# Four-layer network on one core: later weights prepared in nine steps, and attention's norm with tokens on partitions

## The chip, the cores and the metric

The program runs on one NeuronCore of a Trainium2 chip. Five engines share it and work through their own instruction streams, each in order: TensorE (PE: matrix products and transposes, into PSUM), VectorE (DVE), ScalarE (ACT), GpSimd (POOL) and SyncE (SP, which here only starts DMA transfers). They wait for each other through semaphores. The metric is the time of one execution on the device in microseconds (us); less is better.

## What is computed

The input is 4 images of 96 channels, 64 x 64 pixels: 16384 tokens of 96 channels. Four layers follow each other. Layer 0 is a two-layer Mamba block with a pointwise fusion. The change touches layers 1 and 2 and the weights of layers 1 to 3. In short:

```python
# layer 1: depthwise 7x7 convolution, layer norm, MLP
h = conv7x7(x) + conv_b
h = layernorm(h) * ln_g + ln_b
x = x + layer_scale * (gelu(h @ w1 + b1) @ w2 + b2)

# layer 2: attention without softmax, then a feed-forward with fp8 operands
t = tokens(x)                                   # (4, 4096, 96)
q, k, v = split(_ln_t(t) @ Wqkv + bqkv)         # 6 heads of 16
attn = einsum('bhnd,bhmd->bhnm', q, k) * D**-0.5
t = t + einsum('bhnm,bhmd->bhnd', attn, v) @ Wff + bff
t = t + qffn(_ln_t(t))                          # operands rounded to fp8

# layer 3: Fourier mixing over the 4096 tokens, then the same feed-forward
h = relu(bn1(_ln_t(t) @ w1.T))
X = fft(h); y = real(ifft(relu(X * diag + bias)))
t = t + bn2(y @ w2.T)
t = t + qffn(_ln_t(t))
```

`_ln_t` subtracts each token's mean over the 96 channels and divides by the root of its variance plus 1e-5.

## The kernel before

`t` holds the residual stream on chip, 96 channels on partitions and 16384 tokens along them. A block is 512 tokens (`MB`); there are 32 blocks, 8 to a batch (`NB`).

**Order.** In layers 1 to 3 a `manual_schedule` fixes the order of PE, DVE, ACT and POOL as the program is written. SP is not among them: the framework's scheduler places the transfers in SP's queue.

**Layer 1's convolution** (`layer1`, lines 909 to 993). First 16 chunks of `t` are built from layer 0's result (L929 to L933) and transposed into `xt`, which has rows of pixels on 128 partitions. Then 24 groups of four channels run, `g` from 0 to 23. Each group loads a 1 MB band matrix (`load(g)`, L957, three buffers), does 16 matmuls (L983 and L986) into one of four `cv` banks, and evicts four channels, on ACT in even groups (L993) and on DVE in odd ones (L991).

**The later weights** (`consts2`, L821 to L904). Before group 8 the program calls `consts2`, which loads and prepares what layers 1 to 3 need: the MLP's folded bias (three products at L836), its scaled weights, attention's weights, the two feed-forwards' weights rounded to fp8 (L860, L864; both use the same raw buffers `raww1` and `raww2`), the two batch norms folded into `a_w1` and `a_w2` (two products at L899), and the Fourier tables. All of it stands in one place in every engine's order.

**Layer 2** (`layer2`, L1102 to L1217). One loop over slots `j` runs three norms one after the other: of attention (blocks 0 to 31), of the feed-forward (32 to 63), and of layer 3 for the first batch (64 to 71). Each is spread over three slots by `norm_steps`: `center(j)` multiplies by a centring matrix (PE, L1084) and squares (ACT, L1086); `scale(j-1)` sums the squares over channels (PE, L1090) and takes the root by Ln and Exp (ACT, L1092 and L1093); `norm(j-2)` multiplies (DVE, L1096). Channels stay on partitions, so the mean and the root of each token are present on all 96 of them.

Attention is linear, so it needs only the Gram matrix of each batch's normed tokens, with a column of ones for the biases. `turn(j-3)` transposes a normed block to tokens on partitions (PE L1131, ACT L1133), and `products(j-4)` adds it to the Gram matrix (PE L1141). After a batch's last block the five steps of `weights` turn that matrix into one 97 x 96 matrix, through small products (L1147) and copies (L1157 to L1173). `out(j-4-lag)`, with `lag` = `NB` + 3, applies it to a block and adds it to `t` (PE L1179, DVE L1181). The feed-forward's `hidden` (L1236 to L1240) and `project` (L1246 to L1252) begin 35 and 37 slots in.

**Layer 3** (`fourier`) begins with `w1` (PE L1326), which reads all eight normed blocks of the first batch from `h3`.

Names that the prediction uses: `w1raw`, `bn_rows` and `a_w2raw` are raw weights on their way in `consts2`; `cv_ps` the convolution's banks; `xc_ps`, `v_ps` and `rs` the old norm's centred block, its sums of squares and its roots; `av` a tile of layer 3 that ACT scales by a value per partition (L1376); `st` and `mv` layer 1's statistics (L1006, L1007), whose roots are L1011 and L1012, and whose normed block goes back through L1025.

Of the kernel before, what the change touches and what calls it, by code (L numbers as in the profile page):

```python
# [9 lines left out]
F32 = mybir.dt.float32  # L10
# [9 lines left out]
NT = B * L  # L20
# [82 lines left out]
class Net:  # L103
# [715 lines left out]


    def consts2(self, wk, small):  # L821
        tc, nc, ins = self.tc, self.nc, self.ins
        pool = self.pool2

        def load(name, shape, dtype=F32):
            t = pool.tile(shape, dtype, name=name)
            nc.sync.dma_start(t, ins[name])
            return t


        self.c_w1 = load("c_w1", [C, HID])
        self.c_w2 = load("c_w2", [128, 3, C])
        self.c_b1 = pool.tile([128, 3], F32, name="c_b1s")
        ps = small(128, 4)
        for m in range(3):
            nc.tensor.matmul(  # L836
                ps[:, m : m + 1], self.c_w1[:, m * 128 : (m + 1) * 128], self.v("c_ln_b"), start=True, stop=True
            )
        nc.vector.tensor_add(self.c_b1, self.v128("c_b1", 0, 3), ps[:, :3])
        nc.vector.tensor_scalar_mul(self.c_w1, self.c_w1, self.v("c_ln_g"))  # L840
        ls = wk.tile([128, C], F32, name="ls_row")
        nc.sync.dma_start(ls, ins["ls_row"].partition_broadcast(128))
        for m in range(3):
            nc.vector.tensor_mul(self.c_w2[:, m, :], self.c_w2[:, m, :], ls)
        self.c_b2 = pool.tile([C, 1], F32, name="c_b2s")
        nc.vector.tensor_mul(self.c_b2, self.v("c_b2"), self.v("c_ls"))


        self.wkv = load("wkv", [C + 1, 2 * C])
        self.wqt = load("wqt", [C, C + 1])  # L850
        self.wff = load("wff", [C, C])
        self.mask = load("mask", [C, C])


        self.ffn = {}
        for k in ("f2", "f3"):
            a = wk.tile([C, HID], F32, name="w1raw", tag="raww1")
            nc.sync.dma_start(a, ins[f"{k}_w1"])
            w1 = pool.tile([C, HID], F8, name=f"{k}w1q")
            nc.vector.tensor_copy(w1, a, saturate=False)  # L860
            a = wk.tile([128, 3, C], F32, name="w2raw", tag="raww2")
            nc.sync.dma_start(a, ins[f"{k}_w2"])
            w2 = pool.tile([128, 3, C], F8, name=f"{k}w2q")
            nc.vector.tensor_copy(w2, a, saturate=False)  # L864
            b1 = pool.tile([128, 3], F32, name=f"{k}b1q")
            b2 = pool.tile([C, 1], F32, name=f"{k}b2q")
            for b, src in ((b1, self.v128(f"{k}_b1", 0, 3)), (b2, self.v(f"{k}_b2"))):
                q = wk.tile(list(b.shape), F8, name="bq", tag=f"bq{b.shape[0]}{k}")
                nc.vector.tensor_copy(q, src, saturate=False)
                nc.vector.tensor_copy(b, q)  # L870
            self.ffn[k] = (w1, w2, b1, b2)


        self.a_w1 = load("a_w1", [C + 1, NF])
        rows = wk.tile([C + 1, 4, NF], F32, name="bn1_rows")
        nc.sync.dma_start(rows, ins["bn1_rows"].partition_broadcast(C + 1))
        s1 = wk.tile([C + 1, NF], F32, name="bn1_s")
        nc.scalar.activation(s1, rows[:, 3, :], AF.Sqrt, bias=self.eps[: C + 1])
        nc.vector.reciprocal(s1, s1)
        nc.vector.tensor_mul(s1, s1, rows[:, 0, :])  # L880
        nc.vector.tensor_mul(self.a_w1[:C], self.a_w1[:C], s1[:C])
        shift = wk.tile([C + 1, NF], F32, name="bn1_b")
        nc.vector.tensor_mul(shift, s1, rows[:, 2, :])
        nc.vector.tensor_sub(self.a_w1[C:], rows[C:, 1, :], shift[C:])
        r = self.rsqrt(pool, self.v("v2"), "bn2_r")
        self.s2 = pool.tile([C, 1], F32, name="bn2_s")
        nc.vector.tensor_mul(self.s2, r, self.v("g2"))
        self.b2 = pool.tile([C, 1], F32, name="bn2_b")
        nc.vector.tensor_mul(self.b2, self.s2, self.v("m2"))
        nc.vector.tensor_sub(self.b2, self.v("be2"), self.b2)  # L890

        raw = wk.tile([C, NF], F32, name="a_w2raw")
        nc.sync.dma_start(raw, ins["a_w2"])
        gain = wk.tile([C, C], F32, name="bn2_d")
        nc.vector.tensor_scalar_mul(gain, self.ident[:C, :C], self.s2)
        self.a_w2 = pool.tile([C, 2, C], F32, name="a_w2s")
        for half in range(2):
            ps = small(C, C)
            nc.tensor.matmul(ps, raw[:, half * C : (half + 1) * C], gain, start=True, stop=True)  # L899
            nc.vector.tensor_copy(self.a_w2[:, half], ps)  # L900
        self.dft1 = load("dft1", [N1, 2 * 65])
        self.twid = load("twid", [128, 2, 2 * 65])
        self.dft2 = load("dft2", [128, 3 * 128])
        self.dft64 = load("dft64", [128, 2, 128])  # L904

    def layer1(self, scratch, t):
        tc, nc, ins = self.tc, self.nc, self.ins  # L910
# [3 lines left out]
        with ExitStack() as ctx:  # L914
# [4 lines left out]
            with (  # L919
# [48 lines left out]
                def small(rows, cols):  # L968
                    ps = psum.tile([128, 4, 128], F32, name="w_ps", tag="xt", bufs=4)
                    return ps.rearrange("p a c -> p (a c)")[:rows, :cols]  # L970

                x2 = [outer(0)]
                for g in range(C // GC):
                    if g == 8:
                        self.consts2(wk, small)
                    if g % 2 == 0 and g + 2 < C // GC:
                        x2.append(outer(g // 2 + 1))
                    w = load(g)
                    ps = psum.tile([128, GC, B, NR], F32, name="cv_ps", tag="cv", bufs=4)
                    for d in range(GC):  # L980
                        c = g * GC + d
                        for k, j in enumerate((1, 0, 2)):
                            nc.tensor.matmul(  # L983
                                ps[:, d], w[:, d, j], xt[:, c, :, 1 + j : 1 + j + NR], start=k == 0, stop=False
                            )
                        nc.tensor.matmul(ps[:, d], w[:, d, 3], x2[g // 2][:, g % 2 * GC + d], start=False, stop=True)  # L986
                    for d in range(GC):
                        c = g * GC + d
                        dst = xt[:, c, :, 2 : 2 + NR]
                        if g % 2:  # L990
                            nc.vector.tensor_scalar_add(dst, ps[:, d], cb[:, c : c + 1])  # L991
                        else:
                            nc.scalar.activation(dst, ps[:, d], AF.Identity, bias=cb[:, c : c + 1])  # L993
# [82 lines left out]
    def norm_steps(self, t, wk, psum):  # L1076
# [20 lines left out]

        return center, scale, norm

    def layer2(self, t, h3):  # L1102
# [4 lines left out]
        with ExitStack() as ctx:  # L1107
# [9 lines left out]
            for k in range(2):  # L1117
                h = wk.tile([C + 1, L], F32, name=f"h{k}")
                nc.gpsimd.memset(h[C:], 1.0)
                hs.append(h)  # L1120
            ht, gram, g = {}, {}, {}

            def block(i):
                b, s = divmod(i, NB)
                return hs[b % 2][:, s * MB : (s + 1) * MB]

            def turn(i):
                h = block(i)
                ps = psum.tile([128, 4, C + 1], F32, name="ht_ps", tag="ht")
                for d in range(4):  # L1130
                    nc.tensor.transpose(ps[:, d], h[:, d * 128 : (d + 1) * 128], self.ident[: C + 1, : C + 1])  # L1131
                ht[i] = wk.tile([128, 4, C + 1], F32, name="ht", tag="hts", bufs=2)
                nc.scalar.copy(ht[i], ps)  # L1133

            def products(i):
                b, s = divmod(i, NB)
# [45 lines left out]

            lag = NB + 3
            steps = []
            for j in range(2 * n + NB + 2):
                if 0 <= j - 1 < 2 * n + NB:
                    scale(j - 1)
                if j < 2 * n + NB:  # L1190
                    center(j)
                i = j - 2
                if 0 <= i < n:
                    norm(i, block(i)[:C])
                elif n <= i < 2 * n:
                    norm(i, xq(i - n), saturate=False)
                elif i >= 2 * n:
                    norm(i, h3[:C, (i - 2 * n) * MB : (i - 2 * n + 1) * MB])
                if 0 <= j - 4 < n:
                    products(j - 4)  # L1200
                    if (j - 4) % NB == NB - 1:
                        steps = weights((j - 4) // NB)
                else:
                    for f in steps[:1]:
                        f()
                    steps = steps[1:]
                if 0 <= j - 3 < n:
                    turn(j - 3)
                for f in steps[:2]:
                    f()  # L1210
                steps = steps[2:]
                if 0 <= j - 4 - lag < n:
                    out(j - 4 - lag)
                if 0 <= j - n - 5 < n:
                    project(j - n - 5)
                if 0 <= j - n - 3 < n:
# [465 lines left out]
```

## Time and profile before

Three runs took 3753.5, 3758.2 and 3759.5 us, a median of 3758.2.

| | |
|---|---|
| profiled execution: time | 3751.0 us |
| its span | 3749.2 us |
| PE busy | 3115.1 us (83%) |
| DVE busy | 2981.6 us (80%) |
| ACT busy | 2720.5 us (73%) |
| POOL busy | 2566.7 us (68%) |

The profile page cuts the span into 40 slices of 93.7 us and gives the busy share of each engine in tenths (9 is 90% or more), and the TensorE clock that was granted, in tenths of full speed:

```
PE   7887888788878887888887888657799997999888
DVE  5999999999999999999999999931662493444649
ACT  6887888888888888888888888541345685656557
POOL 1899989898999899989989998811001174434527
PEclk8999899899989998999999899658899999999999
```

Layer 0 fills the first 26 slices. The convolution's matmuls run from 2511.0 to 2628.6 us, layer 1's MLP to 2840, layer 2 from there to 3108, layer 3 to the end. "Busy" means that an instruction was executing; a share is an average over stages that have different limits, so what a stage is bound by is read from its own stretch. A wait is given as: engine and line that waited, what ended the wait, us in total, how often, and the longest.

### The profile page before, as it was taken

What the parts mean: (1) busy time and instruction counts of PE and PEld (TensorE: products, weight loads), DVE (VectorE), ACT (ScalarE), POOL (GpSimd) and SP (SyncE); (2) the same over time, 40 slices, a digit from 0 to 9 for tenths busy, and PEclk for the clock granted to TensorE, in tenths of its full rate; (3) what the DMA queues carried; (4) which work ended last, traced back from release to release, by engine and by line L of the source; (5) the groups of instructions that cost most, each with busy time, mean ns of one, the idle gap of its engine ahead of it and who ended that gap; (6) DMA issues with size and microseconds to landing.
All of it is one profiled execution on the core that took longest, in us unless ns stands there. A gap on an engine that the chain in (4) does not pass through costs nothing. (4 is left out here: it accounts for less than half of the span.)

```text
span 3749.2 us, 46836 instructions
## 1 busy us (share of the span) xinstructions
PE 3115.1 (83%) x15326; PEld 1404.9 (37%) x15326; DVE 2981.6 (80%) x2644; ACT 2720.5 (73%) x5456; POOL 2566.7 (68%) x922
## 2 busy tenths in 40 slices
PE   7887888788878887887888888657799997999888
PEld 3232223223222322232233233147344435676643
DVE  5999999999999999999999999931662493444649
ACT  6887888888888888888888888541345685656557
POOL 1899989898999899989989998811001174434527
PEclk8999899899989998999999899658899999999999
DMA  7656665666565666666665666376000000011001
GB/s 187 156 152 160 166 161 148 165 160 172 145 170 152 173 149 169 157 157 161 166 165 142 172 157 173 91 214 217 1 0 1 1 1 6 24 35 46 24 11 57
DMA packets 171644, 446.63 MB, mean 119 GB/s; under 512 B 48756, under 2 KB 50750, under 8 KB 168064
## 3 DMA queue, kind: packets, MB, share of 16 engines
q1 hardware_dynamic: 171400, 443.64, 45.7%
q8 instruction: 121, 1.98, 0.2%
q14 instruction: 123, 1.01, 0.1%
HBM read 369.97 MB, written 73.50 MB: 118 GB/s over the span
## 5 line engine op out<-in xcount | busy, mean ns | idle before, releaser
L648 POOL TENSOR_TENSOR hs<-hs,crep 128x2048 f32<-128x2048 f32 x384 | 1601.2, 4185 | 224.2 <-DVE hs L643 176.4
L610 ACT ACTIVATE da<-ddb,nega 128x1024 f32<-128x1024 f32 x576 | 661.5, 1149 | 197.7 <-DMA ddb<-dd 124.3
L643 DVE TENSOR_TENSOR_SCAN hs<-da,state,rep 128x1024 f32<-128x1024 f32 x288 | 669.2, 2338 | 39.6 <-PE rep L594 21.9
L621 POOL TENSOR_TENSOR up<-udb,brep 128x1024 f32<-128x1024 f32 x192 | 453.0, 2360 | 73.1 <-DMA udb<-ud 58.9
L665 PE MATMUL y<-hs,sel_r 128*32 128x512 f32 x3072 | 459.6, 692 | 12.8 <-POOL hs L648 12.3
L599 PE MATMUL rep<-dbl,sel_b 32*128 32x512 f32 x768 | 250.1, 730 | 215.1 <-DVE hs L643 215.0
L507 ACT ACTIVATE uta<-delta,bt 128x192 f32<-128x192 f32 x1024 | 381.1, 446 | 0.0
L287 PE MATMUL ps<-n,w_x 97*64 97x512 f32 x1536 | 353.8, 602 | 13.0 <-ACT xc L411 12.1
L643 DVE TENSOR_TENSOR_SCAN hs<-da,state,u 128x1024 f32<-128x1024 f32 x144 | 338.1, 2348 | 23.9 <-PE y L665 8.2
L643 DVE TENSOR_TENSOR_SCAN hs<-dap,state,up 128x1024 f32<-128x1024 f32 x144 | 335.2, 2328 | 0.5 <-ACT dap L610 0.5
L594 PE MATMUL rep<-ident,uta 128*128 128x128 f32 x1536 | 222.6, 287 | 105.6 <-DVE hs L643 93.2
L594 PEld LDWEIGHTS rep<-ident,uta 128*128 128x128 f32 x1536 | 174.9, 146 | 246.5 <-issue 133.3
L636 DVE TENSOR_TENSOR u<-udb,rep 128x1024 f32<-128x1024 f32 x192 | 235.4, 1226 | 24.8 <-DMA udb<-ud 11.4
L1240 POOL CAST hq<-y 128x1536 fp8e5<-128x1536 f16 x64 | 94.0, 1469 | 218.1 <-issue 122.6
L643 DVE TENSOR_TENSOR_SCAN hs<-da,rep 128x1024 f32<-128x1024 f32 x96 | 217.9, 2282 | 21.2 <-PE rep L594 14.8
L610 ACT ACTIVATE dap<-ddb,nega 128x1024 f32<-128x1024 f32 x192 | 214.8, 1119 | 24.9 <-DVE hs L643 24.4
L636 DVE TENSOR_TENSOR rep<-udb,rep 128x1024 f32<-128x1024 f32 x192 | 232.0, 1208 | 0.0
L287 PEld LDWEIGHTS ps<-n,w_x 97*64 97x64 f32 x1536 | 103.8, 137 | 260.2 <-issue 210.0
L665 PEld LDWEIGHTS y<-hs,sel_r 128*32 128x32 f32 x3072 | 73.7, 118 | 335.2 <-issue 257.7
L599 PEld LDWEIGHTS rep<-dbl,sel_b 32*128 32x128 f32 x768 | 65.8, 205 | 353.6 <-issue 295.2
L658 PE MATMUL y<-xc,dp 128*128 128x512 f32 x192 | 125.7, 743 | 31.3 <-ACT bt L463 31.3
L1379 POOL TENSOR_TENSOR av<-av,ec 128x780 f32<-128x780 f32 x32 | 58.8, 1837 | 133.7 <-ACT av L1376 133.7
(275 smaller groups left out, 6201.3 us busy)
## 6 DMA issues: line engine op xcount, KB each, us to landing
udb<-ud SPq DMA_DIRECT2D x768, 128.0 KB
ddb<-dd SPq DMA_DIRECT2D x768, 128.0 KB
crep<-cd SPq DMA_DIRECT2D x512, 128.0 KB
dd<-delta SPq DMA_DIRECT2D x64, 384.0 KB
band<-in_band SPq DMA_DIRECT2D x24, 1024.0 KB
ud<-delta SPq DMA_DIRECT2D x62, 384.0 KB
brep<-cd SPq DMA_DIRECT2D x128, 128.0 KB
x<-in_x SPq DMA_DIRECT2D x32, 384.0 KB
```

Source lines behind the costliest of these rows:

```text
L287: nc.tensor.matmul(ps[rows], w[:, 64 * p : 64 * p + 64], rhs[:, at.start + shift : at.stop + shift], start=k == 0, stop=k == len(ws) - 1, ...
L507: nc.scalar.mul(m["uta"][:, q, :, 32 * s4 : 32 * s4 + 32].rearrange("t (p j) d -> t p j d", p=3), m["udt"][:, :, q].rearrange("t p (j d) - ...
L594: nc.tensor.transpose(x[:, q * 128 : q * 128 + 128], made[k]["uta"][:, q, 2 * h + j], self.ident)
L599: nc.tensor.matmul(x[:, at], sel_b[rows, g], made[k]["dbl"][rows, at], start=True, stop=True)
L610: nc.scalar.activation(da, made[k]["dd", h, j], AF.Exp, scale=nega[:, col : col + 1])
L621: nc.gpsimd.tensor_mul(up, made[k]["ud", p][:, j], made[k]["brep", GP])
L636: nc.vector.tensor_mul(u, made[k]["ud", h][:, j], x)
L643: nc.vector.tensor_tensor_scan(hs[:, 1:], made[k].pop(("da", t)), u, st, ALU.mult, ALU.add)
L648: nc.gpsimd.tensor_mul(hs[:, :, :T], hs[:, :, 1:], twice(made[k]["crep", g]))
L658: nc.tensor.matmul(y, dp[:, items[k][2], p], made[k]["xc"][:, p], start=True, stop=True)
L665: nc.tensor.matmul(made[k]["y", p][row : row + 32], sel_r, made[k]["hs", p, g][:, j, at], start=False, stop=True, skip_group_check=True,)
L1240: nc.gpsimd.tensor_copy(q, y2, saturate=False)
```

## The change

`consts2` becomes a generator. It first issues the loads, in four steps; both feed-forwards' raw weights get buffers of their own. Then it does the work on them in five steps. `layer1` takes the steps at groups 4, 5, 6, 7, 14, 15, 16, 17 and 20. The first batch norm's vectors are loaded on one partition (`bn1_rows`, before: broadcast to 97) and reduced there; a product with a row of ones then spreads scale and shift over 97 partitions.

A new `token_norm` does the norm with tokens on partitions, for attention's 32 blocks and for layer 3's first 8. `turn` transposes a raw block of `t` into PSUM (PE) and takes each token's mean and variance there (DVE, four pairs). `root` forms 1/deviation and -mean/deviation, four of each per partition (ACT, ACT, DVE). `times` scales the four pieces (ACT), into one of three tiles that keep a column of ones. `back` transposes the normed pieces to channels on partitions (PE) and copies them out (ACT). The Gram products read the normed tokens directly, so the old `turn` with its copy is gone. The feed-forward's norm stays as it was. `products` moves from `j-4` to `j-2`, `out` from `j-15` to `j-13`, and the loop gets one slot more at its end.

```diff
     def consts2(self, wk, small):
-        def load(name, shape, dtype=F32):
-            t = pool.tile(shape, dtype, name=name)
+        def load(name, shape, dtype=F32, into=pool, key=None):
+            t = into.tile(shape, dtype, name=key or name)
             nc.sync.dma_start(t, ins[name])
             return t
         self.c_w1 = load("c_w1", [C, HID])
         self.c_w2 = load("c_w2", [128, 3, C])
+        ls = wk.tile([128, C], F32, name="ls_row")
+        nc.sync.dma_start(ls, ins["ls_row"].partition_broadcast(128))
+        self.wkv = load("wkv", [C + 1, 2 * C])
+        self.wqt = load("wqt", [C, C + 1])
+        yield
+        self.wff = load("wff", [C, C])
+        self.mask = load("mask", [C, C])
+        raw = {k: load(f"{k}_w1", [C, HID], into=wk, key=f"{k}w1raw") for k in ("f2", "f3")}
+        raw |= {k + "2": load(f"{k}_w2", [128, 3, C], into=wk, key=f"{k}w2raw") for k in ("f2", "f3")}
+        yield
+        self.a_w1 = load("a_w1", [C + 1, NF])
+        rows = wk.tile([1, 4, NF], F32, name="bn1_rows")
+        nc.sync.dma_start(rows, ins["bn1_rows"])
+        araw = load("a_w2", [C, NF], into=wk, key="a_w2raw")
+        self.dft1 = load("dft1", [N1, 2 * 65])
+        yield
+        self.twid = load("twid", [128, 2, 2 * 65])
+        self.dft2 = load("dft2", [128, 3 * 128])
+        self.dft64 = load("dft64", [128, 2, 128])
+        yield
...
+        yield
         self.ffn = {}
         for k in ("f2", "f3"):
-            a = wk.tile([C, HID], F32, name="w1raw", tag="raww1")
-            nc.sync.dma_start(a, ins[f"{k}_w1"])
             w1 = pool.tile([C, HID], F8, name=f"{k}w1q")
-            nc.vector.tensor_copy(w1, a, saturate=False)
-            a = wk.tile([128, 3, C], F32, name="w2raw", tag="raww2")
-            nc.sync.dma_start(a, ins[f"{k}_w2"])
+            nc.vector.tensor_copy(w1, raw[k], saturate=False)
...
+            yield
-        rows = wk.tile([C + 1, 4, NF], F32, name="bn1_rows")
-        nc.sync.dma_start(rows, ins["bn1_rows"].partition_broadcast(C + 1))
-        s1 = wk.tile([C + 1, NF], F32, name="bn1_s")
+        s1 = wk.tile([1, 2, NF], F32, name="bn1_s")
+        one = wk.tile([1, C + 1], F32, name="bn1_one")
+        nc.vector.memset(one, 1.0)
...
+        yield
+        ps = small(C + 1, 2 * NF)
+        nc.tensor.matmul(ps, one, s1.rearrange("p k f -> p (k f)"), start=True, stop=True)
+        nc.vector.tensor_mul(self.a_w1[:C], self.a_w1[:C], ps[:C, :NF])
+        nc.vector.tensor_copy(self.a_w1[C:], ps[C:, NF:])
         self.a_w2 = pool.tile([C, 2, C], F32, name="a_w2s")
...
+        yield
     def layer1(self, scratch, t):
...
+                later = self.consts2(wk, small)
                 for g in range(C // GC):
-                    if g == 8:
-                        self.consts2(wk, small)
+                    if g in (4, 5, 6, 7, 14, 15, 16, 17, 20):
+                        next(later)
...
+    def token_norm(self, wk, tile_of, back_of):
+        nc = self.nc
+        xt, mv, rs, nt = {}, {}, {}, {}
+        kept = [wk.tile([128, 4, C + 1], F32, name=f"nt{k}") for k in range(3)]
+        for k in kept:
+            nc.gpsimd.memset(k[:, :, C:], 1.0)
+        def turn(i, x):
+            ps = xt[i] = tile_of(i)
+            for d in range(4):
+                nc.tensor.transpose(ps[:, d], x[:, d * 128 : d * 128 + 128], self.ident[:C, :C])
+            m = mv[i] = wk.tile([128, 4, 2], F32, name="tmv", tag="tmv", bufs=3)
+            for d in range(4):
+                st = wk.tile([128, 6], F32, name="tst", tag="tst", bufs=4)
+                nc.vector.bn_stats(st, ps[:, d])
+                nc.vector.bn_aggr(m[:, d], st)
+        def root(i):
+            r = rs[i] = wk.tile([128, 2, 4], F32, name="trs", tag="trs", bufs=3)
+            nc.scalar.activation(r[:, 0], mv[i][:, :, 1], AF.Ln, bias=self.eps)
+            nc.scalar.activation(r[:, 0], r[:, 0], AF.Exp, scale=-0.5)
+            nc.vector.scalar_tensor_tensor(r[:, 1], mv.pop(i)[:, :, 0], -1.0, r[:, 0], ALU.mult, ALU.mult)
+        def times(i):
+            n = nt[i] = kept[i % 3]
+            x, r = xt.pop(i), rs.pop(i)
+            for d in range(4):
+                nc.scalar.activation(
+                    n[:, d, :C], x[:, d], AF.Identity, scale=r[:, 0, d : d + 1], bias=r[:, 1, d : d + 1]
+                )
+        def back(i, out):
+            ps = back_of(i)
+            for d in range(4):
+                nc.tensor.transpose(ps[:, d * 128 : d * 128 + 128], nt[i][:, d, :C], self.ident)
+            nc.scalar.copy(out, ps)
+        return turn, root, times, back, nt
     def layer2(self, t, h3):
...
-            ht, gram, g = {}, {}, {}
+            gram, g = {}, {}
+            turn, root, times, back, ht = self.token_norm(
+                wk,
+                lambda i: psum.tile([128, 4, C], F32, name="xt_ps", tag="xc", bufs=3),
+                lambda i: psum.tile([C, MB], F32, name="tp_ps", tag=("v", "ht")[i % 2]),
+            )
...
-            lag = NB + 3
+            lag = NB + 5
-            for j in range(2 * n + NB + 2):
-                if 0 <= j - 1 < 2 * n + NB:
+            for j in range(total + 3):
+                i = j - 2
+                if n <= j - 1 < 2 * n:
                     scale(j - 1)
-                if j < 2 * n + NB:
+                elif token_block(j - 1):
+                    root(j - 1)
+                if n <= j < 2 * n:
                     center(j)
-                i = j - 2
+                elif token_block(j):
+                    turn(j, t[:, j * MB % NT : j * MB % NT + MB])
+                if token_block(j - 1):
+                    times(j - 1)
                 if 0 <= i < n:
-                    norm(i, block(i)[:C])
+                    back(i, block(i)[:C])
...
-                if 0 <= j - 4 < n:
-                    products(j - 4)
+                if 0 <= j - 2 < n:
+                    products(j - 2)
...
-                if 0 <= j - 3 < n:
-                    turn(j - 3)
...
-                if 0 <= j - 4 - lag < n:
-                    out(j - 4 - lag)
+                if 0 <= j - lag < n:
+                    out(j - lag)
```

More of the change, by code (lines that the diff above doesn't have):

```diff
@@ L840, in consts2 @@
         nc.vector.tensor_scalar_mul(self.c_w1, self.c_w1, self.v("c_ln_g"))
-        ls = wk.tile([128, C], F32, name="ls_row")
-        nc.sync.dma_start(ls, ins["ls_row"].partition_broadcast(128))
         for m in range(3):
@@ L846, in consts2 @@
         nc.vector.tensor_mul(self.c_b2, self.v("c_b2"), self.v("c_ls"))
[L849 to L852, printed above, removed]
+        yield
         self.ffn = {}
         for k in ("f2", "f3"):
-            a = wk.tile([C, HID], F32, name="w1raw", tag="raww1")
-            nc.sync.dma_start(a, ins[f"{k}_w1"])
             w1 = pool.tile([C, HID], F8, name=f"{k}w1q")
-            nc.vector.tensor_copy(w1, a, saturate=False)
-            a = wk.tile([128, 3, C], F32, name="w2raw", tag="raww2")
-            nc.sync.dma_start(a, ins[f"{k}_w2"])
+            nc.vector.tensor_copy(w1, raw[k], saturate=False)
             w2 = pool.tile([128, 3, C], F8, name=f"{k}w2q")
-            nc.vector.tensor_copy(w2, a, saturate=False)
+            nc.vector.tensor_copy(w2, raw[k + "2"], saturate=False)
             b1 = pool.tile([128, 3], F32, name=f"{k}b1q")
@@ L871, in consts2 @@
             self.ffn[k] = (w1, w2, b1, b2)
-        self.a_w1 = load("a_w1", [C + 1, NF])
-        rows = wk.tile([C + 1, 4, NF], F32, name="bn1_rows")
-        nc.sync.dma_start(rows, ins["bn1_rows"].partition_broadcast(C + 1))
-        s1 = wk.tile([C + 1, NF], F32, name="bn1_s")
[L878 to L884, printed above, removed]
+            yield
+        s1 = wk.tile([1, 2, NF], F32, name="bn1_s")
+        one = wk.tile([1, C + 1], F32, name="bn1_one")
+        nc.vector.memset(one, 1.0)
+        nc.scalar.activation(s1[:, 0], rows[:, 3, :], AF.Sqrt, bias=self.eps[:1])
+        nc.vector.reciprocal(s1[:, 0], s1[:, 0])
+        nc.vector.tensor_mul(s1[:, 0], s1[:, 0], rows[:, 0, :])
+        nc.vector.tensor_mul(s1[:, 1], s1[:, 0], rows[:, 2, :])
+        nc.vector.tensor_sub(s1[:, 1], rows[:, 1, :], s1[:, 1])
         r = self.rsqrt(pool, self.v("v2"), "bn2_r")
@@ L890, in consts2 @@
         nc.vector.tensor_sub(self.b2, self.v("be2"), self.b2)
-        raw = wk.tile([C, NF], F32, name="a_w2raw")
-        nc.sync.dma_start(raw, ins["a_w2"])
         gain = wk.tile([C, C], F32, name="bn2_d")
         nc.vector.tensor_scalar_mul(gain, self.ident[:C, :C], self.s2)
+        yield
[3 more added lines that the diff above has]
+        nc.vector.tensor_copy(self.a_w1[C:], ps[C:, NF:])
         self.a_w2 = pool.tile([C, 2, C], F32, name="a_w2s")
@@ L898, in consts2 @@
             ps = small(C, C)
-            nc.tensor.matmul(ps, raw[:, half * C : (half + 1) * C], gain, start=True, stop=True)
+            nc.tensor.matmul(ps, araw[:, half * C : (half + 1) * C], gain, start=True, stop=True)
             nc.vector.tensor_copy(self.a_w2[:, half], ps)
[L901 to L904, printed above, removed]
+        yield
     def layer1(self, scratch, t):
@@ L1125, in block @@
                 return hs[b % 2][:, s * MB : (s + 1) * MB]
[L1127 to L1133, printed above, removed]
             def products(i):
@@ L1181, in out, with token_block @@
                 nc.vector.scalar_tensor_tensor(td, ps, self.v("bff"), td, ALU.add, ALU.add)
-            lag = NB + 3
+            lag = NB + 5
             steps = []
-            for j in range(2 * n + NB + 2):
-                if 0 <= j - 1 < 2 * n + NB:
+            total = 2 * n + NB
+            def token_block(i):
+                return 0 <= i < n or 2 * n <= i < total
+            for j in range(total + 3):
+                i = j - 2
+                if n <= j - 1 < 2 * n:
                     scale(j - 1)
-                if j < 2 * n + NB:
+                elif token_block(j - 1):
+                    root(j - 1)
+                if n <= j < 2 * n:
                     center(j)
-                i = j - 2
+                elif token_block(j):
+                    turn(j, t[:, j * MB % NT : j * MB % NT + MB])
+                if token_block(j - 1):
+                    times(j - 1)
                 if 0 <= i < n:
-                    norm(i, block(i)[:C])
-                elif n <= i < 2 * n:
-                    norm(i, xq(i - n), saturate=False)
-                elif i >= 2 * n:
-                    norm(i, h3[:C, (i - 2 * n) * MB : (i - 2 * n + 1) * MB])
-                if 0 <= j - 4 < n:
-                    products(j - 4)
-                    if (j - 4) % NB == NB - 1:
-                        steps = weights((j - 4) // NB)
+                    back(i, block(i)[:C])
+                elif 2 * n <= i < total:
+                    a = (i - 2 * n) * MB
+                    back(i, h3[:C, a : a + MB])
+                if n <= i < 2 * n:
+                    norm(i, xq(i - n), saturate=False)
+                if 0 <= j - 2 < n:
+                    products(j - 2)
+                    if (j - 2) % NB == NB - 1:
+                        steps = weights((j - 2) // NB)
                 else:
```

## The prediction

> **What bounds the kernel now.** I read the page first. Its chain of waits covers only the end of the program, so it says nothing of the two places that the change touches; the 40 slices do: PE is low in slices 25 and 26 and high in the next ten. So I asked for the waits of layer 1's convolution, for the busy time by stretch, and for the instructions in order of time of attention.
>
> Waits in the convolution (engine, line, who ended it: us, times, longest); then stretches (length, busy us and instructions of PE, PE load, DVE, ACT, POOL, granted clock, DMA share, GB/s):
>
> ```profile
> PE w_ps L899 <- DVE bn_d L895: 22.2, 1, 22.2
> DVE f3w1q L860 <- DMA w1raw<-in_f_w: 13.8, 1, 13.8
> ...
> SPq L858 <- DMA bn_rows<-in_bn_rows: 7.4, 1, 7.4
> ...
> 2546.00:2568.00 22.00, 0.00 (x0) 0.01 (x1) 7.73 (x30) 0.64 (x2) 1.45 (x2) 0.59 0.51 172
> ...
> 2590.00:2605.00 15.00, 15.00 (x137) 15.00 (x136) 2.26 (x8) 2.79 (x10) 4.16 (x4) 1.00 0.86 288
> ```
>
> TensorE bounds the convolution: 15.00 us busy of 15, one group of four channels each 3.575 us. In its middle it stands still once, 22.2 us, because all of `consts2` sits before group 8: PE waits in L899 for DVE, DVE for the second `w1raw`, whose buffer and turn in SP's queue came late.
>
> Attention in order of time (start, us, engine, line), one slot with `out`, then the rows that price the new work:
>
> ```profile
> 2889.36 1.02 PE L1090 MATMUL v_ps<-sq,ones 96*96 96x512 f32 x2
> 2890.22 1.02 PE L1084 MATMUL xc_ps<-t,center 96*96 96x512 f32 x2
> 2891.08 0.85 PE L1141 MATMUL gram<-ht 128*97 128x97 f32 x8
> 2891.77 0.50 PE L1131 MATMUL ht_ps<-ident,h 97*128 97x97 f32 x4
> 2892.10 1.02 PE L1179 MATMUL o_ps<-h,g 97*96 97x512 f32 x2
> 2892.96 0.59 PE L1090 MATMUL v_ps<-sq,ones 96*96 96x512 f32 x1
> ```
>
> ```profile
> 2721.70 0.29 DVE L1006 BATCH_NORM_STATS2 st<-xt 128x6 f32<-128x96 f32 x1
> ...
> 2722.12 0.29 DVE L1006 BATCH_NORM_STATS2 st<-xt 128x6 f32<-128x96 f32 x1
> ...
> 2723.08 0.31 ACT L1011 ACTIVATE rs<-mv,eps 128x16 f32<-128x16 f32 x1 [0.88 <-DVE mv L1007]
> ...
> 2723.42 0.22 ACT L1012 ACTIVATE rs<-rs 128x16 f32<-128x16 f32 x1
> ...
> 3137.25 3.67 ACT L1376 ACTIVATE av<-xr_ps,vec 128x65 f32<-128x65 f32 x12
> ```
>
> From start to start the slot's occupancy of PE is 0.86 + 0.86 + 0.69 + 0.33 + 0.86 = 3.60 us, and 3.60 is the slot: PE bounds it. Slots without `out` take 3.02 (starts of L1090 at 2854.01 and 2857.03), with PE waiting for ACT in a loop v, Ln, Exp, Square.
>
> **Part A, the weights in nine steps.** The same 18 loads are issued at groups 4 to 7, and the work on them at 14 to 17 and 20. Ten groups lie between, 36 us, so the wait of L899 goes: -22.2. After the stall three channels ran at 1.70 us where the fourth took 0.87 (half clock, PE having stood): -2.4. Added: one matmul that spreads the two rows, 384 wide, by L1084's 0.86 for 512: +0.65. DVE's steps (largest: reciprocal 1.34, casts and products 0.15 to 0.36 each) and ACT's roots (0.45 and 0.28) move into gaps: each of the two waits 6.0 us before its evictions every 7.15 us, and four `cv` banks let PE run on; without that cover they would cost about 8 us, the sum of the DVE rows.
>
> What is late next is the band. SP issues a band when a group frees its buffer, and the loads stand among them. At 288 GB/s and a share of 0.86 the engines have about 0.17 MB spare per group; 1.76 MB of loads remain (2.04 before, less 0.29 for `bn1_rows`, now one row), a part of them before group 3. SP also sat 4.72 us in one load and 6.70 us in another. Two bands of lead, 7.15 us, swallow most. Bounds 0 and 14 us; I take 3, as the trace's one band wait before the stall is 0.67. A = -22.2 - 2.4 + 0.65 + 3 = **-21 us**.
>
> **Part B, slots 0 to 33 of layer 2.** PE loses v, xc (0.86 each); it keeps the Gram products, transposes 4 blocks in (0.33, as L1131) and 4 back (L1025: 0.11 apart, 0.44): 1.46 without `out`, 2.32 with. PE no longer bounds. The new loop runs over ACT and DVE:
> - root: Ln to Exp 0.34, Exp 0.22, hand-over 0.03, the new [128x4] DVE op 0.16: 0.75. DVE waits here for ACT, which it did not before; behind it stand the next four pairs of statistics and `out`'s addition, and ACT waits for the pairs.
> - then on DVE four pairs 0.42 apart, 1.78 to the end of the last, 0.04 to ACT: 1.82. On ACT four scalings 0.30 apart (L1376: 12 in 3.67) and the copy back, 0.54 (L1086 and its like): 1.78 with the hand-over.
> - `out` on DVE, 0.66, falls into the 0.59 of Ln and Exp: +0.07.
>
> So 2.57 without and 2.64 with `out`: 2.6. Each batch's `weights` steps now cost on ACT: 0.25 + 0.45 waiting + 0.24, then about 1.0 in which the small product waits for DVE behind its statistics, then 0.24: 2.2, 3.5 times = 7.7. Start: GpSimd's ones columns come after two 3.5 us memsets that end at 2846.3, slot 2 wants them at 2845.3: +2 at most with the three short ones. 34 x 2.6 + 7.7 + 2 = 98, against 118.5 (2840.1 to 2958.6): -20.5.
>
> Not in the trace: statistics read from PSUM. The nearest rows are DVE's 128x128 from PSUM (L991, four in 1.13 with 0.34 each: 0.26 apart) and 128x96 from SBUF (L1020, 0.28): no surcharge. [...]
>
> [...] Row: the old slots with 3.88 of 6 us busy (2842 to 2848) were granted 1.00; by the same measure the new ones have 0.50 + 0.60 + 0.85 of 2.6, 75%. But in the token stage, where PE only transposes (15.41 of 31 us), it was granted 0.50 throughout. [...]
>
> **Part C, the rest of layer 2.** Attention's `out` lags 13 slots, not 15: two fewer of the feed-forward slots carry it, 4.98 against 3.45: -3. The eight blocks for layer 3 get worse. Slots 64 to 66 are DVE-bound at 3.45 and now take 1.7 of statistics more, the first two also the last two old norms: 5.3, 5.4, 4.7; then 3.0, 3.0, three of 2.6, and 3.5 for the last root, scaling, return and copy: 32.7. Before: 3082.6 to 3108.2, 25.5. +7. Nothing hides it: layer 3 begins with L1326, which waits for the last block.
>
> **Sum.** -21 - 20.5 - 3 + 7 = -37.5. The profiled execution has a span of 3749.2 and took 3751.0: it becomes 3713.5. The runs shown have a median 7 us higher, 3758.2: **3721**.
>
> **Rivals.**
> - The loop is longer (0.16): PSUM's surcharge and scalings that do not overlap (0.41 each, +0.44) give 3.05 a slot: +17, 3738. For: the loop has four hand-overs, and DVE and ACT are equally long. Against: both pitches are measured.
> - Bands late (0.11): SP sits as long as it did, 14 us waited, 3732. Together with the last: 3749.
> - PE falls to half clock (0.09), the slow side: 13 x 2.90 + 21 x 4.62 + 7.7 + 2 = 144, +26 instead of -20.5: with the rest +9, **3767**. It makes the whole slower once about four fifths of the stage run at half clock. For: the token stage. Against: 1.00 at 65% busy.
> - The stall stays (0.04), because a load is issued late after all: 3742. Against: seven groups between the last load and its first use.
>
> My own case has 0.60 and, with loop 2.45 to 2.75, band waits 0 to 7 and the tail 4 to 10, reaches 3705 to 3735. Faster or slower means by over 0.2% (7.5 us), about what a measurement of this kernel tells from no change. Faster: 0.60 + 0.16 + 0.11 + 0.04, less 0.06 for two mishaps at once, 0.85; same 0.06; slower 0.09. The range 3700 to 3748 leaves out the slow rival.
>
> **What would show it.** No PE wait over 7 us in the convolution, which lasts about 97 us, not 117.6; slots near 2.6 us with DVE and ACT both over 85% busy and clock 1.00; three DVE-bound slots over 4.7 us at the end. Wrong: slots of 3 us or more, a clock of 0.5 in attention, or band waits over 10 us.

## The result, and the profile after

Over four runs each the changed kernel took 3719.2 us (3715.4 to 3723.8), the kernel before 3755.9 us (3749.6 to 3759.5): ratio 0.9905, 95% interval 0.9886 to 0.9923. Measured again later, beside three of the experiments: 3711.8 against 3751.0, ratio 0.9901, interval 0.9887 to 0.9915. The changed kernel is about 1% faster.

The page of the changed kernel (busy shares in tenths over 40 slices, here of 93.0 us):

```profile
span 3722.0 us, 47365 instructions
...
PE   7888788878887888888888878659798888999888
...
DVE  5999999999999999999999999962665693444649
ACT  5888888887888887888888878641346786656557
...
PEclk8999999989999999899999999859899998999989
```

With the slices counted from 1: in slice 28, which is the convolution, PE and the clock are at 9 (before: 7 and 8). DVE has gone from 2 and 4 to 5 and 6 in slices 31 and 32, where attention's statistics now are, and PE from 9 to 8 there. In slice 34, the end of layer 2 and the start of layer 3, the clock is at 8 instead of 9.

A span of 3722.0 against 3749.2 is 27 us, not the 37 of the medians, so the stages have to be read one by one. Each is cut at an instruction of TensorE that stands at the same place in both kernels, and the last row is the changed kernel profiled once more:

| us (granted clock) | to the convolution's first matmul | convolution | to the MLP | MLP | layer 2 to first `hidden` | to layer 3's first `w1` | layer 3 |
|---|---|---|---|---|---|---|---|
| before | 2511.1 | 117.3 (0.86) | 14.4 | 197.3 | 126.3 (1.00) | 141.8 (1.00) | 641.0 |
| after | 2520.0 | 95.1 (0.96) | 14.4 | 197.5 | 108.1 (0.91) | 144.5 (0.94) | 642.3 |
| after, again | 2506.8 | 95.9 (0.94) | 14.5 | 197.3 | 111.4 (0.85) | 144.5 (0.93) | 637.2 |

From the convolution to layer 3 the kernel before takes 597.1 us. The changed one takes 559.7 and 563.6: **37.5 and 33.5 us less**. What lies ahead of the convolution is not touched, and is 9 us longer in one profile and 4 shorter in the other. In all twelve profiles of this study it lies between 2503 and 2520 us.

In the convolution the waits of the changed kernel are (engine, line, who ended it: us, times, longest):

```profile
PE cv_ps L987 <- DMA band<-in_band: 3.0, 2, 2.2
DVE bn_s L887 <- ACT bn_s L886: 2.0, 1, 2.0
...
PEld w_ps L908 <- issue: 0.6, 1, 0.6
```

The 22.2 us wait for `bn_d` is gone; two waits for a band, 3.0 us together, are what is late next.

In attention, two stretches of the changed kernel (length, busy us and instructions of PE, PE load, DVE, ACT, POOL, granted clock, DMA share, GB/s), four plain slots and the slots after batch 2's last block:

```profile
2840.50:2850.50 10.00, 9.02 (x66) 6.01 (x64) 6.06 (x36) 8.97 (x28) 0.00 (x0) 1.00 0.01 2
...
2900.00:2911.00 11.00, 10.65 (x51) 7.78 (x50) 4.96 (x22) 5.17 (x18) 0.00 (x0) 0.59 0.00 0
```

And one plain slot with `out`, ScalarE in order of time:

```profile
2913.23 0.31 ACT L1123 ACTIVATE trs<-tmv,eps 128x4 f32<-128x4 f32 x1
2913.57 0.21 ACT L1124 ACTIVATE trs<-trs 128x4 f32<-128x4 f32 x1
2914.01 1.40 ACT L1131 ACTIVATE nt<-xt_ps,trs 128x96 f32<-128x96 f32 x4 [0.23 <-DVE trs L1125]
2915.29 0.58 ACT L1139 COPY h<-tp_ps 96x512 f32<-96x512 f32 x1
2915.75 0.31 ACT L1123 ACTIVATE trs<-tmv,eps 128x4 f32<-128x4 f32 x1
```

The slot is 2.52 us, from Ln to Ln. ScalarE has no other gap of note in it than the 0.23 us until VectorE's product -mean/deviation: ACT bounds these slots (8.97 of 10 us), and DVE is busy for only 6.06 of 10. In the second stretch it is PE that is busy (10.65 of 11) at a clock of 0.59, and both others wait. Before that the clock was 1.00, and in the 3.41 us ahead of the drop PE was busy for 1.35 only, waiting for the first copy of the `weights` steps:

```profile
2895.44:2898.85 3.41, 1.35 (x13) 0.96 (x10) 2.46 (x12) 3.15 (x10) 0.00 (x0) 1.00 0.00 0
```

How DVE and then ACT wait in the second stretch, in order of time:

```profile
2901.30 0.75 DVE L1221 SCALAR_TENSOR_TENSOR t<-o_ps,vec,t 96x512 f32<-96x512 f32 x1 [2.99 <-PE o_ps L1219]
2901.97 0.15 DVE L1125 SCALAR_TENSOR_TENSOR trs<-tmv,trs 128x4 f32<-128x4 f32 x1
```

```profile
2902.16 1.40 ACT L1131 ACTIVATE nt<-xt_ps,trs 128x96 f32<-128x96 f32 x4 [1.90 <-DVE trs L1125]
```

DVE stands 2.99 us at `out`'s addition, for PE; the product of the next root is behind it in DVE's order, and ACT's scalings wait 1.90 us for that.

### The profile page after: what moved, and what is told of

It is laid out like the page before. It is cut to its first block, busy times and chain, and to the rows that moved or that the text cites. A ratio compares the mean times of both kernels' runs of the same rounds, so it can differ in the third digit from the quotient of the medians.

```text
span 3722.0 us, 47365 instructions
## 1 busy us (share of the span) xinstructions
PE 3098.0 (83%) x15360; PEld 1409.3 (38%) x15360; DVE 3020.9 (81%) x2966; ACT 2722.6 (73%) x5584; POOL 2567.9 (69%) x925
```

## The experiments

Kernels that differ from the change by a few us are compared by the stages of their profiles, since the untouched stage ahead of the convolution alone moves by 17 us. Lengths are from the convolution's first matmul on, cut as in the table above.

**The first part taken back** (`e1_weights_in_one_place`):

```diff
-                later = self.consts2(wk, small)
...
-                    if g in (4, 5, 6, 7, 14, 15, 16, 17, 20):
-                        next(later)
+                    if g == 8:
+                        self.consts2(wk, small)      # with the body of before
```

> The change with its first part undone: consts2 is called once, at group 8, as before; the new norm stays. Theory (the parts are independent, as in the prediction, and the first part is worth 21 to 22 us): the 22 us wait for f3's raw weights is back in the convolution, its matmuls last 117 us again, and layer 2 keeps its gain of 15.5 us: about 3741, which is 22 above the changed kernel and 15 below the one before. Rival 1 (what the convolution gained was paid back elsewhere, so that undoing it costs less than 15 us): 3731 or less. Rival 2 (the first part also cost the 9 us by which the convolution's first matmul came later in the changed kernel's profile): about 3732, with that first matmul at 2511 and not at 2520.

3736.1 us (ratio to before 0.9957, 0.9943 to 0.9971). The convolution takes 116.8 us, 20.9 more than in the repeated profile of the change. The two stages of layer 2 are the same to 0.1 us as there (111.4 and 144.5). Rival 2 falls: the first matmul came at 2519.4. The median is 5 us under the expected 3741, between theory and rival 1; the stages decide for the theory.

**The first part alone** (`e2_weights_steps_alone`: before, with the nine steps and the new `consts2`).

> The first part of the change alone: nine steps over the convolution, layer 2 as before. Theory: the convolution lasts 95 to 97 us, everything after it is as long as before: 22 us below the kernel before, about 3734. Rival 1 (the first part pays its gain back): above 3741. Rival 2 (it also costs 9 us ahead of the convolution): about 3743, the convolution's first matmul at 2520.

3732.0 us (0.9945, 0.9932 to 0.9958), 23.5 below before. The convolution takes 93.8 us, a little under the expected 95 to 97, layer 2 126.3 and 142.1, as before: the whole gain sits in the one stage, and layer 2 pays nothing back. Its band waits were 2.2 us. Both rivals fall: nothing is paid back, and the first matmul came at 2512.3.

**All loads at one group** (`e11_loads_at_once`), one execution:

```diff
-                    if g in (4, 5, 6, 7, 14, 15, 16, 17, 20):
-                        next(later)
+                    if g in (4, 14, 15, 16, 17, 20):
+                        for _ in range(4 if g == 4 else 1):
+                            next(later)
```

> The changed kernel with all 18 loads of the weights issued at group 4 instead of over groups 4 to 7; the work on them stays in its five steps. Theory (the loads delay the bands behind them in SP's queue; spread over four groups that cost one wait of 2.2 to 2.3 us, and 2.0 MB at some 290 GB/s are 7 us, about the lead of two bands): one or two waits of TensorE for a band, 4 to 9 us in total, the convolution 97 to 102 us instead of 95 to 96. Rival (the scheduler places the loads in SP's queue by its own reckoning, so that the group at which the program issues them changes nothing): 95 to 96 us and a wait of 2 to 3 us, as in the changed kernel.

The convolution takes 99.4 us, 3.5 to 4.3 more than with loads spread out. The waits of this kernel in the convolution, PE's row for a band:

```profile
PE cv_ps L988 <- DMA band<-in_band: 4.0, 2, 3.8
```

The wait is at the low end of what the theory gave and the length in the middle: the place of the loads counts, by a few us. The longer wait explains 1 to 2 us of the 4 (the change: 3.0 and 2.3 us). Behind it the clock was at half, here from 2532.6 to 2539.5. Two stretches of this kernel:

```profile
2535.00:2540.00 5.00, 5.00 (x28) 5.00 (x28) 0.00 (x0) 0.00 (x0) 0.00 (x0) 0.56 0.52 215
2540.00:2545.00 5.00, 5.00 (x47) 5.00 (x46) 0.94 (x4) 1.15 (x4) 0.92 (x1) 1.00 0.67 221
```

28 matmuls run in 5 us at 0.56 where 47 run at 1.00. At half clock 6.83 us cost some 3.4, by estimate; behind the waits of the change it was 3.41 us in the repeated profile and none in the first. Wait and clock together give the 3.5 to 4.3.

**The old norm for layer 3's eight blocks** (`e3_last_eight_old_norm`):

```diff
             def token_block(i):
-                return 0 <= i < n or 2 * n <= i < total
+                return 0 <= i < n
...
-                if n <= j - 1 < 2 * n:
+                if n <= j - 1 < total:
                     scale(j - 1)
...
-                if n <= j < 2 * n:
+                if n <= j < total:
                     center(j)
...
-                    back(i, h3[:C, a : a + MB])
+                    norm(i, h3[:C, a : a + MB])
```

> The changed kernel with the old norm, channels on partitions, for the eight blocks of layer 3 (slots 64 to 71); attention keeps the new one. Theory (the tail costs what the prediction said, or a little more, 7 to 10 us, since VectorE is the bound in slots 64 to 66): 7 to 10 us less than the changed kernel, about 3710; from the first norm of those blocks to layer 3 about 25 us, as before. Rival (the tail is hidden, or the old norm gives the time back through its longer loop of 3.0 us a slot): within 2 us of the changed kernel, about 3719.

3700.9 us (0.9861, 0.9848 to 0.9874). From the first `hidden` to layer 3 it takes 137.1 us instead of 144.5: the new norm costs **7.4 us** in the tail. The median fell further than that. The profile has 2507.4 us ahead of the convolution, 12.6 less than the first profile of the change, and 105.2 us in attention, where the change had 108.1 and 111.4; neither is an effect of the edit, which touches neither stage.

**`out` fifteen slots behind** (`e10_lag_15`: `lag = NB + 7`), one execution.

> The changed kernel with attention's out fifteen slots behind its block, as before, instead of thirteen. Theory (each feed-forward slot that carries out takes about 5.0 us and each that doesn't 3.45, so two slots more cost 3 us): ten slots of about 5.0 instead of eight, the feed-forward part of layer 2 about 147.6 us instead of 144.5 from its first hidden product to layer 3. Rival (out is hidden in whichever slot it stands, and the pitch there comes from something else): 144.5 as before.

147.6 us, as the theory said: the two slots fewer are worth 3.1 us.

**Statistics in PSUM** (`e5_statistics_in_psum`). In the changed kernel's tail, slots 65 and 66 last 7.57 and 6.83 us from Ln to Ln. Around the first of them, DVE and then POOL in order of time:

```profile
3050.23 0.87 DVE L1289 TENSOR_SCALAR y<-y,f2b1q 128x512 f16<-128x512 f16 x3
3051.01 2.54 DVE L1125 SCALAR_TENSOR_TENSOR trs<-tmv,trs 128x4 f32<-128x4 f32 x1
3053.48 0.25 DVE L1118 BATCH_NORM_STATS2 tst<-xt_ps 128x6 f32<-128x96 f32 x1
```

```profile
3050.39 1.74 POOL L1302 TENSOR_TENSOR t<-t,z 96x512 f32<-96x512 f32 x1 [1.56 <-DVE z L1300]
3052.08 1.46 POOL L1290 CAST hq<-y 128x1536 fp8e5<-128x1536 f16 x1
```

A product of four elements per partition takes 2.54 us, and ends when GpSimd's cast ends (3052.08 + 1.46 = 3053.54). In slot 66 it is the same: 2.54 us from 3057.37, until a cast that ends at 3059.89. Over the kernel's 40 blocks this product's median is 0.16. Both its operands are in SBUF. That this is why it lasts as long as GpSimd's work beside it is the author's guess, not shown by this trace; with one operand in PSUM 0.2 us was expected in both slots, and a tail some 4 us shorter. The edit moves one operand, and widens the PSUM tile from 96 to 128 columns a piece to make room for it:

```diff
-            ps = xt[i] = tile_of(i)
+            tile = tile_of(i)                    # [128, 4, 128]
+            ps = xt[i] = tile[:, :, :C]
...
-            m = mv[i] = wk.tile([128, 4, 2], F32, name="tmv", tag="tmv", bufs=3)
+            m = mv[i] = tile[:, :, C : C + 2]
```

> The changed kernel with mean and variance written into the PSUM tile of the block instead of SBUF, so that the product -mean/deviation (L1125) has one operand in SBUF, not two. [...] Rival 2 (PSUM makes the small operations longer, 40 slots by 0.1): slower by 4.

3706.7 us against 3711.8 of the change beside it; the ranges overlap (3701.3 to 3719.4 and 3709.3 to 3716.2). The profile is clear. The same place in this kernel, DVE and then POOL:

```profile
3040.37 0.15 DVE L1126 SCALAR_TENSOR_TENSOR trs<-xt_ps,trs 128x4 f32<-128x4 f32 x1
```

```profile
3039.74 1.72 POOL L1303 TENSOR_TENSOR t<-t,z 96x512 f32<-96x512 f32 x1 [2.06 <-DVE z L1301]
3041.41 1.46 POOL L1291 CAST hq<-y 128x1536 fp8e5<-128x1536 f16 x1
```

GpSimd runs without a break from 3039.74 to 3042.87, and the product takes 0.15 us while it runs. Slots 65 and 66 last 5.18 and 4.94 us, 4.3 less together. So the long product goes with the edit; by what mechanism, the run does not show. Rival 2 holds as well: a pair of statistics now takes 0.525 us from start to start instead of 0.365, and the plain slot 2.70 instead of 2.52; whether that comes from writing to PSUM or from the wider tile was not separated. The two nearly cancel in the time.

**The copy ahead of the scalings** (`e4_copy_before_scalings`):

```diff
-                if token_block(j - 1):
-                    times(j - 1)
                 if 0 <= i < n:
                     back(i, block(i)[:C])
...
+                if token_block(j - 1):
+                    times(j - 1)
                 if n <= i < 2 * n:
                     norm(i, xq(i - n), saturate=False)
```

> The changed kernel with the return and its copy ahead of the four scalings in ScalarE's order (the change has them last). Theory 1 (ScalarE sets the slot of 2.52 us and stands 0.23 us of it waiting for VectorE's -mean/deviation; the copy of an older block fills that wait): slots of about 2.3 us, 0.2 less in some 34 to 40 slots, 7 to 9 us less than the changed kernel, about 3711. Theory 2 (the loop over VectorE and ScalarE sets the slot, statistics, Ln, Exp, product, statistics; the order on ScalarE is free): slots stay at 2.5 us, about 3719. Theory 3 (the copy delays the scalings, and TensorE's return waits for them): slots of 2.8 us, about 3729.

3706.0 us (0.9877, 0.9862 to 0.9892). A slot of this kernel, ScalarE in order of time:

```profile
2829.75 0.30 ACT L1123 ACTIVATE trs<-tmv,eps 128x4 f32<-128x4 f32 x1
2830.08 0.20 ACT L1124 ACTIVATE trs<-trs 128x4 f32<-128x4 f32 x1
2830.26 0.58 ACT L1139 COPY h<-tp_ps 96x512 f32<-96x512 f32 x1
2830.75 1.39 ACT L1131 ACTIVATE nt<-xt_ps,trs 128x96 f32<-128x96 f32 x4
2832.02 0.30 ACT L1123 ACTIVATE trs<-tmv,eps 128x4 f32<-128x4 f32 x1
```

2.27 us (2.31 in slots with `out`), and no wait is left: theory 1. Layer 2's first stage takes 98.3 us, 9.8 to 13.1 less than in the change, and 6.8 less than in the kernel with the old norm for layer 3, whose attention is the change's, with more clock. Of that, 16 plain slots give 3.6 us. The twelve slots of the `weights` steps after batches 0 to 2 take 36.4 us at a clock of 1.00, against 40.1 there and 43.0 and 46.4 in the change, and three slots at the start are 1.0 longer. The clock was at 1.00 in these twelve slots in the profile of the pieces together too, and below that with the old order and attention unaltered: in the four slots after batch 2 it was 0.70 in both profiles of the change, and 0.88 in the kernel with the old norm for layer 3. That the exchange keeps it up is likely, but no run tests it alone.

**One needless product in the slots of the weights steps** (`e8_extra_product`). Batches are counted from 0 here, from 1 in the expectation. In the two profiles of the change the same four slots after a batch's last block took 14.3 or 17.0 us after batch 1, 17.1 in both after batch 2; they are long where the clock was granted at 0.5 (after batch 2 from 2898.85 to 2909.00 in the first profile). The edit gives TensorE 0.65 us more to do in the slots `j` % 8 = 2, 3, 4:

```diff
+            if warm:
+                nc.tensor.matmul(
+                    ps.rearrange("p d c -> p (d c)")[:C], self.center, x[:, : 4 * C], start=True, stop=True
+                )
             for d in range(4):
                 nc.tensor.transpose(ps[:, d], x[:, d * 128 : d * 128 + 128], self.ident[:C, :C])
```

> The changed kernel with one needless product, 384 wide (0.65 us), ahead of the block's transposes in the slots that follow a batch's last block, batches 1 to 3; its result is overwritten. Theory (TensorE's half clock after an idle stretch sits on the chain of the weights steps: the same four slots took 17.1 us at clock 0.50 to 0.59 and 14.3 us where it was granted 0.72 to 1.00): the clock stays at 1.00 in these slots and they take 13 to 14.5 us, so that layer 2 is 2 to 5 us shorter than in the changed kernel beside it. Rival 1 (TensorE has slack there, so its clock doesn't matter and the difference came from elsewhere): slots as before, 14 to 17 us, or longer by 0.65 each. Rival 2 (one product is too little to keep the clock): 0.5 still there, nothing gained.

The slots after batch 2, first in the repeated profile of the change, then in this kernel (columns as in the stretches above):

```profile
2886.70:2903.80 17.10, 14.63 (x78) 10.67 (x78) 8.88 (x42) 9.79 (x33) 0.00 (x0) 0.70 0.00 0
```

```profile
2887.40:2901.20 13.80, 11.16 (x80) 8.00 (x79) 8.73 (x40) 9.66 (x33) 0.00 (x0) 1.00 0.00 1
```

With more instructions PE is busy 3.5 us less, at a clock of 1.00 instead of 0.70, and the four slots take 13.9 us instead of 17.1. After batch 1 they take 15.4, between the 14.3 and 17.0 of the change. After batch 0 they take 14.3 instead of 11.6 and 12.3: there the product only cost. With 0.44 more in one later slot after batches 1 and 2, the stage is 1.9 us shorter than in the repeated profile, just short of the expected 2 to 5, and 1.4 longer than in the first. The median (3715.1) doesn't tell it from the change.

That the product kept the clock after batch 2 is not shown. The kernel with statistics in PSUM, which has no such product, was granted 1.00 in these slots too and took 13.9 us; the one with the old norm for layer 3, which has the change's attention, took 14.3 at 0.88:

```profile
2884.81:2899.10 14.29, 11.83 (x80) 8.61 (x79) 8.90 (x42) 9.78 (x34) 0.00 (x0) 0.88 0.00 0
```

What these profiles show together is that half clock is on the path here: the same slots of the same code take 14.3 us at a mean clock of 0.88, or 17.1 at 0.70. An added product is no good remedy.

**The pieces together** (`e9_best`: the edits of `e3` and `e4`, and the long memsets moved behind those of the ones columns).

> The old norm for layer 3's eight blocks, the copy ahead of the scalings, and the ones columns of the three kept tiles set before the two long memsets. Theory (the pieces add: 8.8 us of tail, 11.3 of attention by the stages' lengths, of which 1.5 in the tail are lost, and 1.5 to 2 us of TensorE's wait for the ones columns): 540 us from the convolution's first matmul to layer 3's first, against 597 before and 560 with the change; median about 3698 to 3700. Rival (they overlap, since both relieve the same loop): 546 or more, median 3705.

3693.4 us; ratio to before 0.985, interval 0.9836 to 0.9863, against 0.9887 to 0.9915 of the change on the same chip. From the convolution to layer 3 it takes 94.9 + 14.4 + 195.5 + 96.3 + 137.1 = 538.2 us, where 540 was expected. This version beats both kernels.

**The change unaltered once more** (`after_again`), whose values were used above.

> The changed kernel once more, unaltered, beside the next three. It tells what the time ahead of the convolution does by itself: nothing there was touched, yet the convolution's first matmul came at 2511.1 (before), 2520.0 (the change), 2519.4, 2512.3, 2507.4 and 2503.4 us in six profiles. Theory (it varies from run to run): this profile has another value than 2520.0, the time from the convolution's first matmul to layer 3's first is again within 2 us of the 559.7 of the first profile, and the median is 3712 to 3722. Rival (the change delays it): 2518 to 2522 again, median 3719 or more.

The stage ahead of the convolution took 2506.8 us: it varies by itself, and the rival falls. The median, 3711.8, lies just under the expected 3712. The rest, 563.6, is 3.9 us off the 559.7 of the first profile, not within 2. Most of the difference is the clock in attention: after batch 1 the four slots took 17.0 us at a mean clock of about 0.7, in the first profile 14.3 at about 0.9.

## Why the prediction held, step by step

- **Part A, -21.** -22.2 (95.1), -21.4 (95.9) and, with the part alone, -23.5 (93.8). The wait of L899 went, and the restart at half clock behind it (before: 0.58 from 2568 to 2575 us; in the repeated profile 3.4 us of half clock came behind the band wait). One or two band waits came, of 2.2 to 3.0 us in total: the 3 us taken between 0 and 14 were right. It was the list of waits that found the stall: the low slices 25 and 26 that the prediction names are counted from 0 and lie mostly ahead of the convolution. That the loads can be late, the rival of 0.11, is real only if they stand together, and then it costs 4 us, not 11 more, half of it or more by the clock.
- **Part B, -20.5.** Measured -18.2 and -14.9, and -21.1 with the change's attention in the kernel with the old norm for layer 3, where more clock was granted. By the prediction's own cut, slots 0 to 33, the change takes 101.3 and 104.6 us and that kernel 98.3, where 98 were expected. So it is met where the clock was kept best, and was too large by 2 to 6 us in the change, with two errors that partly cancel.
  - *The loop, 2.57 and 2.64*: 2.52 in both. It was built as a chain over both engines, in which DVE's four pairs stand between two roots. The chain of the changed kernel is ACT's own sequence: a pair takes 0.365, not 0.42, so that DVE is done before ACT. That DVE would be over 85% busy is wrong (61%); that the copy's place in ACT's order costs 0.2 to 0.25 a slot was not seen.
  - *The weights steps, 2.2 a batch*: batches 0, 1 and 2 cost 1.5, 4.2 and 7.1 us over plain slots of 2.52, in the repeated profile 2.2, 6.9 and 7.0. This is the term that was mis-sized. It counted only ACT's waits for small products. In the trace DVE's `out` addition waits up to 3.0 us for its product on PE, which stands behind the small products there; the root's product stands behind the addition, and the scalings behind that. PE's part of this is longer at half clock: after batch 2 ACT waited 1.39 us for the product that L1209 copies in both profiles of the change, and 0.49 at a clock of 1.00, in the kernel with the extra product.
  - *No surcharge for statistics from PSUM*: right, `bn_stats` takes 0.23 from PSUM, where layer 1's takes 0.29 from strided SBUF. The surcharge in the rival of the longer loop is shown by no run; the loop took 2.52 us with the statistics read from PSUM. (The rival's longer loop, 3.05, would by its own figures have cost 34 x 0.45 = 15 us, not 17.)
  - *Clock 1.00*, and the rival of half clock (0.09): neither. In plain slots away from the start and a batch's end it is 1.00. The stage as a whole was granted 0.91 and 0.85, and a clock of 0.5 in attention was on the prediction's own list of signs of being wrong. The rival's error was to let the clock fall for whole stages; it falls after the half-idle stretch of a batch's end (PE busy for 1.35 of 3.41 us), for 3.4 to 10.2 us at a time, and where it stays down longest it costs 2.8 us a batch more. The 2.90 and 4.62 us a slot in the rival's sum are shown by no run: plain slots took 2.52 with `out` and without, and the four slots after batch 2 took 17.1 at a mean clock of 0.70, 4.3 each.
- **Part C.** *The lag, -3*: 3.1. *The tail, +7*: 7.4. The sum was right by luck, its working was not: slots 64 and 65, from statistics to statistics on DVE, last 6.4 us, not 5.3 and 5.4, since the product takes 2.54 us in both and ends with GpSimd's cast. The later slots were put too high (4.3, 2.7, 2.6, 2.5 for 4.7, 3.0, 3.0, 2.6), and the errors cancel.
- **Sum, -37.5.** By stages 37.5 and 33.5 less, by medians 36.6 and 39.2. That the first is the forecast to the digit is luck: part B fell short, and part C came to +2.7 where +4 was expected. The step from the profiled execution to the median, +7, lies within the 17 us by which the untouched stage ahead of the convolution varies; the forecast of 3721 depends on it.

## What to carry to other kernels

When work moves from one engine to others, write down each engine's sequence for one slot and sum it; the longest sequence and the longest loop of waits both bound the slot, and a gap inside the longest sequence is worth filling with work that is already ready (0.2 to 0.25 us in each slot here, by exchanging two calls). A norm that is good in one stage can be bad in the next: the same code gained in attention and cost 7.4 us where VectorE was the bound already. Preparations that stand in one place of every engine's order are worth spreading as soon as one of their loads is late, with several groups between load and use, and with the loads themselves spread out.

## What the hardware showed that was not expected

- A VectorE product of 128x4 with both operands in SBUF took 2.54 us beside GpSimd's addition and cast (1.74 and 1.46 us), and 0.15 with one operand in PSUM, beside the same work (1.72 and 1.46).
- Writing mean and variance to PSUM, in a wider tile, made a pair of statistics 0.525 us from start to start, from 0.365, though the single instructions grew only from 0.23 to 0.27 and from 0.18 to 0.19 us.
- TensorE was granted half clock in attention though it was busy for 90% of the plain slots; the drops lie at a batch's end and at the stage's start. How long it lasts differs between two executions of the same program: 14.3 or 17.0 us for the same four slots. With the same code attention took 105.2 to 111.5 us. In the first profile of the change PE was busy for 33, 38 and 40% of the 3.41 us ahead of its three drops; a stretch as long after batch 0, with 38% (1.28 us from 2849.50), was followed by no drop.
